# Two blocks of tokens scattered per step at the end of a chunk, and its slabs begun sooner: a GRU followed by a mixture of experts on one Trainium2 core

## The chip, the cores and the metric

The kernel runs on one core of a Trainium2 chip. The metric is the device time of one execution in microseconds, the median of several runs. The core has a matrix engine (PE), a vector engine (DVE), a scalar engine (ACT), a general engine (POOL) and a sync engine (SP). In this kernel SP issues nearly all plain DMAs, and POOL issues the indirect ones, whose rows are addressed by an index tile. Each engine takes its instructions in the order in which the program has them; an instruction that waits holds back all that stand behind it on that engine.

## The reference

A GRU runs over 256 time steps for 16 sequences of width 512. Each of the 4096 hidden states then goes through 8 low-rank experts of rank 128, of which two are kept, weighted by a normalised softmax of a router. The result is added to the input.

```python
def cell(h, x):
    gi = x @ W_ih + b_ih
    gh = h @ W_hh + b_hh
    i_r, i_z, i_n = jnp.split(gi, 3, axis=-1)
    h_r, h_z, h_n = jnp.split(gh, 3, axis=-1)
    r = jax.nn.sigmoid(i_r + h_r)
    z = jax.nn.sigmoid(i_z + h_z)
    n = jnp.tanh(i_n + r * h_n)
    h_new = (1.0 - z) * n + z * h
    return (h_new, h_new)
...
router_logits = x / norm @ router_w
routing_weights = softmax(router_logits)
rw, selected_experts = jax.lax.top_k(routing_weights, 2)
rw = rw / jnp.sum(rw, axis=-1, keepdims=True)
combine = sum over the two of one_hot(selected_experts, 8) * rw
out = sum over e of combine[:, e, None] * (x @ Wa[e] @ Wb[e])
x = x + out
```

## The kernel before

**The recurrence.** The outer loop has 32 blocks of 8 time steps; step `now` counts from 1 to 256. A step (function `step`) multiplies the hidden state by `W_hh` on PE into the banks `rn` (L914) and `z` (L924). ACT computes `r` (L940), `z` (L945) and `n` (L949), DVE the products around them (L947, L948, L952, L954, L956), and a DVE transpose (L959) turns the new state into `hist`, the left side of the next step's matmuls. Beside it PE multiplies the inputs of a later pair of steps by `W_ih` (L281, L289). ACT copies biases into the banks ahead of that (`seed`, L261). For the twelve pairs of steps in `EARLY` the input products are computed far ahead (class `Early`), so that in those steps PE has more time for the experts. Inputs are loaded a block at a time, eight DMAs on SP (`load_x`, L132).

**The experts.** The first 29 blocks are grouped in four chunks of 7, 11, 7 and 4 blocks. A block is 128 tokens. The last three blocks take a dense path over all experts (class `Moe`). For a block of a chunk, class `Route` issues these, a step or more apart: `keep` stores the block's states to DRAM (`H`, eight DMAs on SP, L597); `fetch` loads them back as rows of tokens (`ht`, on SP, L605), in the same piece as the router's logits; `norm` has ACT square and sum them (L620) and POOL take the root by a power (`nrm`, L622); `soft1` is the softmax on DVE and ACT; `soft2` picks two experts on DVE (`top2`; POOL fills the end of its tile `pr` by a memset, L319, before DVE's max, L324, may read it).

After the last block of a chunk, class `Chunk` places its tokens. It ranks them by expert (`ranks`, `places`, `experts`, `weights`, on PE and DVE). Then it moves every block's tokens into slots sorted by expert: `fetch(m)` loads the 128 tokens of block m from `H` into one of two `ht2` buffers (a 256 KB DMA on SP, L545), and `scatter(m)` writes them to the DRAM tensor `x_slots`, once for each of the two experts (two indirect DMAs on POOL, L551). `fetch(m + 2)` needs the buffer of block m back, so it waits until both scatters of m have landed.

The slots are then worked through in slabs of 128 (class `Slab`): four DMAs on SP load one (`xg`, L652), when all scatters of the chunk have landed; POOL copies its expert's weights (`wag`, `wbg`, L670, L674); DVE transposes it (L680); PE multiplies it down (L691) and up (L706) in four half pieces; ACT copies the result out (L714) and SP stores it (L715). When a chunk's slabs are done, class `Combine` gathers two rows per token (POOL, L743), loads the residual `xr` (SP, L739), adds both (DVE, L757) and stores the output (SP, L761).

**The planner.** Each of these classes gives a list of `Piece`s in its `plan`: a gap in steps to the piece before it, a cost in microseconds of PE, the PE work, the other operations (`then`), and the buffers it takes and gives. In each step `choose` takes what may come, in the order of `place`: chunks and routing at 0, in the order in which they began, slabs next, combines, dense blocks, early inputs last. Slabs and dense blocks have a due step, and a running credit spreads their cost up to it. PE work goes behind the step's own matmuls, the other operations behind the step's end. All engines' orders are then fixed as written. `ready[c]` is the step at which chunk c's slabs begin, and a chunk's slabs are due at `ready[c + 1] + 5`:

```python
ready = [e + LAG + k for e, k in zip(ends, CHUNKS)]
```

After step 256 the planner goes on, with more PE work per step, until all is done.

Of the kernel before, what the change touches and what calls it, by code (L numbers as in the profile page):

```python
# [23 lines left out]
CHUNKS = [7, 11, 7, 4]  # L24
LAG = 10
# [19 lines left out]
def gru_moe_kernel(  # L45
# [49 lines left out]
    E, _, R = wa.shape  # L95
# [263 lines left out]
    class Early:  # L359
# [55 lines left out]
        def plan(self):  # L415
            pieces = [
                Piece(then=[("load",)], takes="early"),
                Piece(gap=2, then=[("turn",)], takes="at"),
            ] + [
                Piece(gap=0, cost=c, pe=[("into", what, q)])  # L420
                for what, c in (("rn", 0.43), ("z", 0.22))
                for q in range(NQ)
            ] + [Piece(then=[("store",)], gives="early")]
            pieces[2].gap, pieces[2].takes = 1, ["ps"]
            pieces[9].then, pieces[9].gives = [("keep",)], ["ps", "at"]
            return pieces


    class Chunk:
# [139 lines left out]
        def plan(self):  # L569
            k = self.k  # L570
            pieces = [
                Piece(gap=7, cost=0.9, pe=[("ranks",)],
                      then=[("places",), ("places2",)]),
                Piece(then=[("places3",)]),
                Piece(then=[("experts",)]),
                Piece(then=[("weights",)]),
            ] + [Piece() for _ in range(k - 2)]
            pieces[0].then[:0] = [("fetch", m) for m in range(2)]
            for m in range(k):
                pieces[2 + m].then.append(("scatter", m))  # L580
                if m + 2 < k:
                    pieces[2 + m].then.append(("fetch", m + 2))
            return pieces

    class Route:
# [414 lines left out]
    starts = {}  # L1000
    room = dict(ROOM)
    ends = [TS * sum(CHUNKS[: c + 1]) for c in range(len(CHUNKS))]
    ready = [e + LAG + k for e, k in zip(ends, CHUNKS)]
    n_slabs = [(2 * P * k + (P - 1) * E) // P for k in CHUNKS]

    def at_step(n, make):
# [99 lines left out]
    for i in range(NB):  # L1106
        rows, rows_next = rows_next, None
        for t in range(TS):
# [3 lines left out]
            m = i * NM + t // 2  # L1112
# [20 lines left out]
        if i < n_sparse:  # L1133
            ch = chunks[-1]
            k = i - (ends[ch.c] // TS - ch.k)
# [55 lines left out]
```

## Time and profile before

| | us |
|---|---|
| median of 3 runs | 1308.48 (1308.43 to 1308.65) |
| the profiled execution | 1301.67 |
| its span, first to last instruction | 1299.9 |
| PE, DVE, ACT, POOL busy | 1252.2, 734.4, 391.4, 285.4 |
| first `r` (L940) of the recurrence, and last | 37.26, 1216.89 |
| last matmul ends | 1289.84 |

The mean granted clock of PE was 0.992. All times in the profile are of one execution and count from its first instruction. A line of the timeline gives the start, the duration, the engine, the source line, the operation, what it writes and reads, how many instructions it stands for, and in brackets how long the engine was idle before it and what ended that wait. A line of the waits names the waiting engine and line, what it waited for, and the total, the number and the longest of these waits. SPq is SP's queue of DMA issues: the duration there is that of issuing, not of the transfer.

### The profile page before, as it was taken

The numbers are of one execution on the slowest core, as the hardware profiler recorded it, in microseconds if no ns is written. First come the engines' busy times: TensorE is split into PE (matmuls) and PEld (weight loads), VectorE is DVE, ScalarE is ACT, GpSimd is POOL, SyncE is SP. The second block draws the span as 40 slices with busy tenths as digits, with TensorE's granted clock in tenths as the row PEclk, the third lists the DMA queues.
The fourth block names the chain that finished last, engine by engine and source line by source line (L and its number), as shares of the span: only waits on it lengthen the run. The fifth ranks groups of instructions, "written<-read, shape, count | busy, mean of one in ns | idle before, by whom it ended". The sixth has DMA issues, their size and how long they took to land. (4 is left out here: it accounts for less than half of the span.)

```text
span 1299.9 us, 68450 instructions
## 1 busy us (share of the span) xinstructions
PE 1252.2 (96%) x30378; PEld 888.0 (68%) x30378; DVE 734.4 (56%) x2678; ACT 391.4 (30%) x1354; POOL 285.4 (22%) x504
## 2 busy tenths in 40 slices
PE   6799999999999999999999999999999999999996
PEld 2477777777777777777777766777777777777652
DVE  1445555555555555555556646666556556676643
ACT  1222232222223333233232323333333333333320
POOL 2000000000421100000100433232114234373552
PEclk7999999999999999999999999999999999999999
DMA  8522322321522221112111544655335446774786
GB/s 196 158 98 86 103 91 80 104 92 47 191 77 62 60 61 54 49 44 60 43 56 57 193 153 122 173 163 150 97 98 184 150 134 183 207 224 144 206 256 179
DMA packets 149477, 158.67 MB, mean 122 GB/s; under 512 B 22646, under 2 KB 103606, under 8 KB 149180
## 3 DMA queue, kind: packets, MB, share of 16 engines
q1 hardware_dynamic: 139760, 123.83, 32.2%
q0 software_dynamic: 9280, 30.42, 7.5%
q8 instruction: 238, 3.90, 1.3%
q14 instruction: 59, 0.48, 0.1%
q10 hardware_dynamic: 140, 0.05, 0.0%
HBM read 84.21 MB, written 69.99 MB: 119 GB/s over the span
## 5 line engine op out<-in xcount | busy, mean ns | idle before, releaser
L914 PE MATMUL rn<-whh,hist 128*32 128x256 f32 x8160 | 493.6, 382 | 19.4 <-DVE hist L959 16.5
L914 PEld LDWEIGHTS rn<-whh,hist 128*32 128x32 f32 x8160 | 247.7, 110 | 201.4 <-DVE hist L959 51.8
L281 PE MATMUL rn<-wih,xT 128*32 128x256 f32 x3712 | 287.9, 381 | 11.3 <-DMA wih<-in_L_cond_W_ih_dram 9.4
L947 DVE SCALAR_TENSOR_TENSOR n<-r,rn 128x128 f32<-128x128 f32 x256 | 73.2, 286 | 362.2 <-ACT r L940 361.2
L924 PE MATMUL z<-whh,hist 128*32 128x128 f32 x8160 | 271.0, 273 | 0.0
L924 PEld LDWEIGHTS z<-whh,hist 128*32 128x32 f32 x8160 | 235.5, 110 | 42.9 <-issue 0.4
L940 ACT ACTIVATE r<-rn 128x128 f32<-128x128 f32 x256 | 70.9, 277 | 426.4 <-PE rn L914 426.4
L289 PE MATMUL z<-wih,xT 128*32 128x128 f32 x3712 | 188.4, 274 | 0.0
L289 PEld LDWEIGHTS z<-wih,xT 128*32 128x32 f32 x3712 | 122.0, 111 | 80.4 <-issue 1.8
L281 PEld LDWEIGHTS rn<-wih,xT 128*32 128x32 f32 x3712 | 112.0, 110 | 12.9 <-DMA wih<-in_L_cond_W_ih_dram 5.1
L945 ACT ACTIVATE z<-z 128x128 f32<-128x128 f32 x256 | 71.0, 278 | 151.1 <-PE z L924 150.5
L952 DVE SCALAR_TENSOR_TENSOR zh<-z,h 128x128 f32<-128x128 f32 x255 | 77.7, 305 | 65.6 <-ACT z L945 65.4
L622 POOL TENSOR_TENSOR nrm<-ss,half 128x1 f32<-128x1 f32 x29 | 16.2, 560 | 411.5 <-ACT ht L620 392.4
L691 PE MATMUL at_ps<-xgT,wag 128*32 128x128 f32 x2752 | 96.8, 273 | 2.2 <-POOL nrm L808 1.4
L706 PE MATMUL y_ps<-wbg,at 128*32 128x256 f32 x1376 | 94.6, 380 | 0.8 <-ACT at L698 0.8
L691 PEld LDWEIGHTS at_ps<-xgT,wag 128*32 128x32 f32 x2752 | 79.1, 110 | 9.8 <-issue 3.1
L959 DVE STREAM_TRANSPOSE hist<-rows 128x128 f32<-128x128 f32 x256 | 79.8, 312 | 8.7
L967 DVE STREAM_TRANSPOSE h<-hist 128x128 f32<-128x128 f32 x256 | 79.7, 311 | 8.7
L956 DVE SCALAR_TENSOR_TENSOR rows<-zh,m 128x128 f32<-128x128 f32 x256 | 76.0, 297 | 8.9
L674 POOL COPY wbg<-wb_sb 128x512 f32 x86 | 55.4, 644 | 114.9 <-PE y_ps L706 114.9
L949 ACT ACTIVATE n<-n 128x128 f32<-128x128 f32 x256 | 77.3, 302 | 7.6 <-DVE n L948 7.3
L714 ACT COPY y<-y_ps 128x512 f32<-128x512 f32 x86 | 50.1, 583 | 94.9 <-PE y_ps L706 85.7
(136 smaller groups left out, 1050.4 us busy)
## 6 DMA issues: line engine op xcount, KB each, us to landing
xg<-x_slots SPq DMA_DIRECT2D x344, 64.0 KB
y_slots<-y SPq DMA_DIRECT2D x86, 256.0 KB
ht<-H SPq DMA_DIRECT2D x58, 256.0 KB
x_slots<-zero SPq DMA_DIRECT2D x50, 256.0 KB
x<-in_x_dram SPq DMA_DIRECT2D x256, 32.0 KB
xr<-in_x_dram SPq DMA_DIRECT2D x32, 256.0 KB
out_dram<-xr SPq DMA_DIRECT2D x32, 256.0 KB
H<-rows SPq DMA_DIRECT2D x232, 32.0 KB
```

The source lines that it names most:

```text
L281: pe.matmul(rn[32 * j : 32 * j + 32, 0 : 3 * P].rearrange("p (g d) -> p g d", g=3)[:, 0:3:2, :], lhsT=xts[m][:, q, :], rhs=w[:, 0:3:2, j, ...
L289: ins = pe.matmul(zb[32 * j : 32 * j + 32, 0:P], lhsT=xts[m][:, q, :], rhs=w[:, 1, j, :], start=False, stop=(q == NQ - 1), skip_group_chec ...
L691: pe.matmul(self.ps[c32, 0:P], lhsT=self.wa[:, q, c32], rhs=self.xt[:, q, :], start=(q == 0), stop=(q == NQ - 1),)
L706: pe.matmul(self.ps[c32, half], lhsT=self.at[:, c32], rhs=self.wb[:, half], start=True, stop=True,)
L914: pe.matmul(rn[32 * j : 32 * j + 32, 0 : 2 * P].rearrange("p (g d) -> p g d", g=2), lhsT=hT[:, q, :], rhs=w(q, j)[:, 0:3:2, :], start=Fals ...
L924: pe.matmul(zb[32 * j : 32 * j + 32, 0:P], lhsT=hT[:, q, :], rhs=w(q, j)[:, 1, :], start=False, stop=(q == NQ - 1), skip_group_check=True,)
L947: dve.scalar_tensor_tensor(n, r, 1.0, rn[:, P : 2 * P], ALU.add, ALU.mult)
L949: act.activation(n, n, AF.Tanh)
L952: dve.scalar_tensor_tensor(zh, z, 1.0, hrow, ALU.add, ALU.mult)
L956: dve.scalar_tensor_tensor(hn, zh, 0.5, m, ALU.mult, ALU.subtract)
L959: dve.transpose(hist[:, t, :, lo : lo + 32], hn.rearrange("p (q c) -> p q c", q=NQ))
L967: dve.transpose(hrow.rearrange("p (q c) -> p q c", q=NQ), hT)
```

## The change

The scatters of two blocks, with the two fetches that reuse their buffers, now stand in one piece, where each block had a piece of its own. The plan of a chunk of k blocks has (k + 1) // 2 - 2 empty pieces behind the first four instead of k - 2. A chunk's slabs begin k - (k + 1) // 2 steps sooner: 3, 5, 3 and 2 steps. The due step of each chunk's slabs moves with the next chunk's start.

```diff
-            ] + [Piece() for _ in range(k - 2)]
+            ] + [Piece() for _ in range((k + 1) // 2 - 2)]
             pieces[0].then[:0] = [("fetch", m) for m in range(2)]
             for m in range(k):
-                pieces[2 + m].then.append(("scatter", m))
+                pieces[2 + m // 2].then.append(("scatter", m))
                 if m + 2 < k:
-                    pieces[2 + m].then.append(("fetch", m + 2))
+                    pieces[2 + m // 2].then.append(("fetch", m + 2))
             return pieces
...
-    ready = [e + LAG + k for e, k in zip(ends, CHUNKS)]
+    ready = [e + LAG + (k + 1) // 2 for e, k in zip(ends, CHUNKS)]
```

The two operations that are moved, as they stand in the kernel:

```python
def fetch(self, k):
    ht = moe.tile([P, D], FP, tag="ht2", bufs=2, name=f"ht2_{self.c}_{k}")
    sp.dma_start(ht, self.rows[k].rearrange("b t d -> (b t) d"))
...
def scatter(self, k):
    for ix in self.idx:
        ins = pool.indirect_dma_start(
            out=self.x[:, :],
            out_offset=bass.IndirectOffsetOnAxis(ap=ix[:, k : k + 1], axis=0),
            in_=self.ht[k][:, :],
...
```

## The prediction

> **What bounds the kernel now.** I read the page first, then the waits, then the timeline row by row at the end of each chunk, then the chain. The page and the two longest waits on ACT and DVE:
>
> ```profile
> PE 1252.2 (96%) x30378; PEld 888.0 (68%) x30378; DVE 734.4 (56%) x2678; ACT 391.4 (30%) x1354; POOL 285.4 (22%) x504
> ACT r L940 <- PE rn L914: 426.4, 248, 3.9
> DVE n L947 <- ACT r L940: 361.2, 237, 4.9
> ```
>
> PE has work nearly always, and the recurrence hands each of the 256 steps on in turn (PE, ACT `r`, DVE `n`, ACT, DVE, PE). The starts of `r` (L940) run from 37.26 to 1216.89 us. With at most one half slab piece (cost 0.43 in the plan) a step takes 4.41 us; two take 4.77, three 5.20, four about 5.65. So beside the input-gate matmuls a step lasts about max(4.41, 3.91 + cost): the loop has some 0.5 us of free PE time, and all beyond is paid. ACT and DVE obey their own order: whatever makes either wait stops the step.
>
> What the change touches is not on PE. Waits on POOL and on SP's queue (total us, times, longest):
>
> ```profile
> POOL x_slots L551 <- DMA ht<-H: 49.8, 16, 6.9
> SPq L545 <- DMA x_slots<-ht,ilo: 57.9, 12, 12.6
> ```
>
> POOL's scatter waits for its block's fetch, SP's fetch waits for a scatter. It is a loop through the two `ht2` buffers: scatter m must have landed before fetch m+2 may be issued, and that before scatter m+2. The timeline of POOL and SP in chunk 1:
>
> ```profile
> 717.01 1.04 POOL L551 DMA_INDIRECT x_slots<-ht,ihi  x1 [8.31 <-DVE ilo L507]
> 718.36 0.99 POOL L551 DMA_INDIRECT x_slots<-ht,ilo  x1 [0.30 <-issue]
> ...
> 726.10 1.00 POOL L551 DMA_INDIRECT x_slots<-ht,ihi  x1 [3.09 <-DMA ht<-H]
> ...
> 735.74 0.59 POOL L622 TENSOR_TENSOR nrm<-ss,half 128x1 f32<-128x1 f32 x1
> ...
> 743.48 0.14 POOL L319 MEMSET pr<- 128x6 f32 x1
> 722.35 0.32 SPq L545 DMA_DIRECT2D ht<-H  x1
> 722.77 5.46 SPq L597 DMA_DIRECT2D H<-rows  x8
> ```
>
> Scatter 0 leaves POOL at 719.35, fetch 2 is issued at 722.35 (3.0 us), scatter 2 starts at 726.10 (3.75 us). Over the chunk the first gap lies between 1.8 and 3.3 us, the second between 3.55 and 5.1, long beside the H stores. I take 2.6 and 3.9 (5.0 beside H stores). With 2.25 us of POOL for a pair of scatters the loop takes 2.25 + 2.6 + 3.9 = 8.75 us for two blocks, 4.4 a block: just the length of a step. The old plan, one block a step, is already at that rate. And the loop once stops the recurrence, at step 164 (7.31 us between its `r` and the next), when the next block's `ht` fetch stood behind it on SP:
>
> ```profile
> 773.17 0.63 ACT L620 ACTIVATE ht<-ht 128x512 f32<-128x512 f32 x1 [4.14 <-DMA ht<-H]
> ```
>
> **The change part by part.** The number of scatters, fetches, matmuls and bytes is the same. Two blocks a step are asked of a loop that yields one. By the order of the changed program's instructions, a chunk's queues look so: on SP, fetches 2 and 3 now precede the next block's eight H stores (L597), fetches 4 and 5 its `ht` fetch (L605), 8 and 9 (of the 11-block chunk) an x load. On POOL, the next block's `nrm` power (L622) stands behind scatter 6 (chunks 0, 2) or 7 (chunk 1) instead of behind 3; its `pr` memset (L319) in chunk 1 behind scatter 10 instead of 5. ACT's Square (L620) waits for that `ht`, DVE's softmax for `nrm`, DVE's max (L324) for `pr`; ACT and DVE are the recurrence.
>
> *Chunk 1 (11 blocks).* From scatter 0 at 717.0: fetch 2 at 722.35, fetch 3 at 724.5, H stores 724.9 to 730.4 (5.5 us as in the row), fetch 4 at 731.0; scatter 3 at 729.6 to 731.9, fetch 5 at 734.5, the `ht` fetch at 734.9, landing at 737.5 (it took 2.6 us before: 731.30 to 733.87). ACT then needs 2.35 us for Square, a `y` copy and the seeds: `r` of step 157 at 739.85 in place of 736.8, 3.05 us lost. Scatters 4 to 7 start at 734.9, 738.4, 743.7, 747.2, so `nrm` is ready at 750.2 and `n` of step 158 starts at 751.5, not 741.46: 10.0 us lost in all. Scatters 8, 9 and 10 end at 754.8, 758.3 and 764.0 (fetch 10 waits for SP's x load until 757.8). Then `pr`, 0.95 us of top-two on DVE, and `n` of step 159 at 765.3 in place of 745.88. **+19.4 us.** The stall at step 164 goes, because the block's fetch then finds SP free: 7.31 to 4.41, **-2.9.**
>
> *Chunk 0 (7 blocks).* Fetch 2 at 328.4 and scatter 2 at 332.2 as now; fetch 3 331.7, H stores to 338.0, fetch 4 338.0, fetch 5 341.1, `ht` fetch 341.5, landing 344.4 against 341.25: 3.1 us. Scatter 4 from 341.9 to 344.2, fetch 6 346.8, scatter 6 from 350.7 to 353.0, `nrm` 353.6, softmax 1 us: `n` of step 70 at 354.8 in place of 347.7. **+7.1.**
>
> *Chunk 2 (7 blocks).* The same chain from 982.28 brings `nrm` to 1012.2. But these steps carry slab work and take 5.1 to 5.6 us, so the recurrence comes later and waits less: `ht` costs 0.5, `nrm` 3.5. **+4.0.**
>
> *Chunk 3 (4 blocks)* has no routed block behind it; scatter 3 now ends near 1155.5, and the slab weights behind it on POOL (near 1157) are needed by PE near 1166. **0**, with bounds -1 (a 5.94 us step near there loses its excess) and +2 (one weight late).
>
> *Slabs begun sooner.* The plan now begins them at steps 71, 161, 215, 245 in place of 74, 166, 218, 247. Summing max(4.41, 3.91 + cost) over both plans (2.18 in place of 3.91 where no input gates are computed) gives 5.2 us more in the recurrence; the work after step 256 falls from 66.7 to 62.4, and PE is busy there nearly throughout (L863, L826, L691, L706 end to end), so 4.3 comes back. **+0.9.** This is the whole PE effect of the head start: work moved from one full place to another.
>
> *The end.* PE's last matmul ended at 1289.84, but the span at 1299.9. The chain says why:
>
> ```profile
> 1282.81 5.35 DMA out_dram<-xr
> 1288.15 0.02 issue
> 1288.17 4.24 DMA xr<-in_x_dram
> ```
>
> The last residual tile was loaded late, behind two Combine outputs, and Combines 27 and 28 ended after it. In the new plan these two stand 3 steps before, but the last `xr` load still waits behind their outputs on SP. From the starting time of the last block's routing I get 18.2 us to its landing (Combine outputs 5.35, loads 4.24, adds 0.74 each) against 16.4 for PE, then 0.7 and 4.6 us for add and output: 23.6 where it now is 26.4. **-2.8**, bounds -5 (load not late at all) and 0.
>
> The trace cannot show two pairs of scatters with two fetches issued in one step. From below, transfers could be no slower than the shortest gaps (1.8 and 3.55: loop 7.6 us), from above they crowd (3.3 and 4.7: 10.3 us). A rule weighs against my size: the Trainium skill, "DMA: Bandwidth & Descriptors", section "Anatomy of one DMA", puts a DMA at about 2.0 us plus its bytes at 436 GB/s. For 256 KB that is an estimate of 2.6 us, so 2.25 + 2.6 + 2.6 = 7.45 us a loop. The first gap agrees, the second is measured at 3.75 where the rule says 2.6. By the rule chunk 1 would lose 12.5, chunk 0 3, chunk 2 0.5, and the sum be +11. I take the rows, and keep the rule as the near end.
>
> Sum: 7.1 + 19.4 - 2.9 + 4.0 + 0 + 0.9 - 2.8 = **+25.7 us.** The profiled execution took 1301.67 us (span 1299.9), 6.8 under the median of the runs, 1308.48; I carry the difference over: 1334.2.
>
> **The rivals.**
> - *Short loop.* Fetches in pairs land as the rule says: +11, 1319.5. For it: gaps of 1.8 us occur. Against: the second gap was never under 3.55.
> - *Long loop.* Scatters, fetches, H stores and x loads crowd one another at 10.3 us a loop or more: 1.6 us more per loop, five loops in chunk 1 (8 us), three in chunk 0 (5) and three in chunk 2 (some 3, the rest hidden), so 16 more, 1350. For it: 5.1 us beside the H stores.
> - *Faster: the queue does not hold.* If POOL never waited for a fetch, a pair would cost it 2.55 us, 11 blocks 28 us, and `pr` would be ready at 745, when DVE wants it. Then only -2.9, +0.9 and -2.8 remain: -4.8, 1303.7. It decides from a loop under some 5.1 us for two blocks; every row speaks for over 7.
> - *No head start at all.* The slabs begin 3 to 5 steps sooner, but these steps come later on the clock: step 161 would be at 773.8, step 166 was at 779.3. In that case the -2.8 at the end falls away too: 1337. It is within the forecast's range.
>
> **How the numbers follow.** Forecast with its near variant 0.74, short loop 0.11, long loop 0.09, faster 0.03, no difference (short loop and a full gain at the end) 0.03. Low 1318 takes in the rule, high 1347 the larger part of the long loop. About 0.2% (2.6 us) is what a measurement of this kernel can tell from no change: faster 0.03, same 0.03, slower 0.94.
>
> **What would show it.** In the profile after: POOL waiting for `ht<-H` before most scatters, for 3 to 5 us; `nrm` (L622) and `pr` (L319) directly behind a scatter; DVE waiting for `nrm` near steps 69, 157 and 213, and for `pr` at step 158, by about 7 and 9 us in chunk 1; the 7.31 us step gone; PE's share of the span lower. Wrong would be: no DVE wait for POOL at these steps, a loop under 7 us, or chunks 0 to 2 longer by less than 10 us in all.

## The result, and the profile after

| | before | after |
|---|---|---|
| median of six runs each, us | 1308.57 (1305.98 to 1310.31) | 1346.22 (1342.87 to 1348.98) |
| profiled execution, us | 1301.67 | 1346.27 |
| its span, us | 1299.9 | 1344.5 |
| mean granted clock of PE | 0.992 | 0.978 |

The ratio is 1.0298 (1.0282 to 1.0314); the two medians stand 37.7 us apart, where 25.7 were forecast. The profiled executions stand 44.6 apart, because that of before lay 7 us under its median and that of after did not; below, the terms are those of the profiled executions.

The page and the waits of the kernel after (total us, times, longest), and below them two waits of the kernel before:

```profile
PE 1264.1 (94%) x30378; PEld 894.9 (67%) x30378; DVE 738.3 (55%) x2678; ACT 391.7 (29%) x1354; POOL 286.6 (21%) x504
POOL x_slots L551 <- DMA ht<-H: 49.0, 16, 6.6
DVE rn L301 <- POOL nrm L622: 19.0, 3, 8.3
DVE m L324 <- POOL pr L319: 17.9, 3, 13.1
ACT ht L620 <- DMA ht<-H: 11.9, 3, 5.7
```

```profile
ACT ht L620 <- DMA ht<-H: 6.4, 4, 4.1
DVE m L324 <- POOL pr L319: 1.3, 2, 0.8
```

The first wait, POOL on the fetches, is as long as before (49.8). What has changed is who waits for POOL and SP in turn: DVE for `nrm` and `pr`, ACT for `ht`. Together these waits are 48.8 us, three times each. Before, ACT's wait for `ht` was 6.4 us, DVE's for `pr` 1.3, and one for this `nrm` was not in the list. The timeline of POOL and DVE in chunk 1 (start, duration, engine, line, what; in brackets the idle time before):

```profile
759.98 0.97 POOL L551 DMA_INDIRECT x_slots<-ht,ilo  x1 [0.30 <-issue]
760.97 0.59 POOL L622 TENSOR_TENSOR nrm<-ss,half 128x1 f32<-128x1 f32 x1
...
776.57 0.97 POOL L551 DMA_INDIRECT x_slots<-ht,ihi  x1 [6.61 <-DMA ht<-H]
777.85 0.97 POOL L551 DMA_INDIRECT x_slots<-ht,ilo  x1 [0.31 <-issue]
778.79 0.15 POOL L319 MEMSET pr<- 128x6 f32 x1
761.59 0.15 DVE L301 TENSOR_SCALAR rn<-nrm 128x1 f32<-128x1 f32 x1 [8.34 <-POOL nrm L622]
...
778.97 0.17 DVE L324 MAX8 m<-pr 128x8 f32<-128x14 f32 x1 [13.08 <-POOL pr L319]
```

A memset of 0.15 us, queued behind the eleventh scatter, holds DVE for 13.08 us and with it the recurrence. The small instructions that the forecast named stand where it put them. Not in the forecast is what the idle time does to PE. Four stretches of 6 us in chunk 1 (length, then busy PE, PEld, DVE, ACT, POOL with their instructions; granted clock, DMA share, GB/s):

```profile
730.00:736.00 6.00, 6.00 (x184) 4.67 (x180) 4.63 (x19) 0.75 (x3) 2.17 (x3) 1.00 0.60 187
760.00:766.00 6.00, 2.22 (x32) 1.38 (x36) 3.50 (x15) 1.95 (x8) 3.00 (x4) 0.51 0.59 157
778.00:784.00 6.00, 1.57 (x16) 0.79 (x20) 3.53 (x16) 0.31 (x1) 2.36 (x5) 0.50 0.23 87
790.00:796.00 6.00, 6.00 (x160) 4.55 (x156) 1.98 (x7) 1.73 (x7) 0.00 (x0) 1.00 0.26 77
```

In the two stretches with a stall the granted clock was 0.51 and 0.50, in the two others 1.00. The timeline of PE has it at the next state product:

```profile
782.43 3.64 PE L914 MATMUL rn<-whh,hist 128*32 128x256 f32 x32 [11.82 <-DVE hist L959]
```

The same 32 matmuls take 1.93 us elsewhere. The kernel before has one such slow product, near its start:

```profile
65.51 3.02 PE L914 MATMUL rn<-whh,hist 128*32 128x256 f32 x32 [3.78 <-DVE hist L959]
```

The end has a queue of its own. POOL, then DVE and PE, in the last dense block, and below them the same last product in the kernel before:

```profile
1325.71 1.00 POOL L743 DMA_INDIRECT yg<-y_slots,ilo  x1 [0.30 <-issue]
1326.69 0.13 POOL L319 MEMSET pr<- 128x6 f32 x1
1326.86 0.18 DVE L324 MAX8 m<-pr 128x8 f32<-128x14 f32 x1 [4.66 <-POOL pr L319]
1328.81 1.97 PE L847 MATMUL aT_ps<-ident,a 128*128 128x128 f32 x8 [6.74 <-DVE a L838]
1330.70 8.46 PE L863 MATMUL o_ps<-wb_sb,aT 128*32 128x512 f32 x64
```

```profile
1282.76 7.08 PE L863 MATMUL o_ps<-wb_sb,aT 128*32 128x512 f32 x64
```

The gathers of Combines 27 and 28 now stand ahead of this block's `pr` on POOL. PE idles 6.74 us and then takes 8.46 us for the product that took 7.08 before. The two Combines are early now, and the end after the last matmul is 5.3 us instead of 10.1; but the last matmul itself comes late.

### The profile page after: what moved, and what is told of

It is laid out like the page before. It is cut to its first block, busy times and chain, and to the rows that moved or that the text cites. A ratio compares the mean times of both kernels' runs of the same rounds, so it can differ in the third digit from the quotient of the medians.

```text
span 1344.5 us, 68453 instructions
## 1 busy us (share of the span) xinstructions
PE 1264.1 (94%) x30378; PEld 894.9 (67%) x30378; DVE 738.3 (55%) x2678; ACT 391.7 (29%) x1354; POOL 286.6 (21%) x504
## 4 chain that ended last, share of the span: by engine, by line
PE 79%; DMA 8%; issue 5%; DVE 3%; POOL 2%; SPq 1%; ACT 1%; POOLq 0%; ACTq 0%; DVEq 0%
PE rn L914 31%; PE z L924 15%; PE rn L281 13%; PE z L289 6%; PE y_ps L706 4%; PE at_ps L691 4%; DMA x_slots<-ht,ilo 3%; DMA ht<-H 2%; PE gi L387 1%; POOL x_slots L551 1%; DMA wih<-in_L_cond_W_ih_dram 1%; DMA whh<-in_L_cond_W_hh_dram 1%; PE rt L353 1%; POOL yg L743 1%; DMA wb_sb<-in_L_ffn_Wb_dram 1%
## 5 line engine op out<-in xcount | busy, mean ns | idle before, releaser
L914 PE MATMUL rn<-whh,hist 128*32 128x256 f32 x8160 | 499.6, 386 | 31.4 <-DVE hist L959 29.4
L914 PEld LDWEIGHTS rn<-whh,hist 128*32 128x32 f32 x8160 | 252.1, 111 | 216.1 <-DVE hist L959 63.5
L281 PE MATMUL rn<-wih,xT 128*32 128x256 f32 x3712 | 289.3, 383 | 14.6 <-ACT rn L261 7.4
L281 PEld LDWEIGHTS rn<-wih,xT 128*32 128x32 f32 x3712 | 112.2, 111 | 16.5 <-ACT rn L261 8.2
L948 DVE SCALAR_TENSOR_TENSOR n<-n,rn 128x128 f32<-128x128 f32 x256 | 73.6, 287 | 8.7
```

Of the source, the lines that this page charges most:

```text
L281: pe.matmul(rn[32 * j : 32 * j + 32, 0 : 3 * P].rearrange("p (g d) -> p g d", g=3)[:, 0:3:2, :], lhsT=xts[m][:, q, :], rhs=w[:, 0:3:2, j, ...
L914: pe.matmul(rn[32 * j : 32 * j + 32, 0 : 2 * P].rearrange("p (g d) -> p g d", g=2), lhsT=hT[:, q, :], rhs=w(q, j)[:, 0:3:2, :], start=Fals ...
L948: dve.scalar_tensor_tensor(n, n, 0.5, rn[:, 2 * P : 3 * P], ALU.mult, ALU.add)
```

## The experiments

Eight kernels were run in two groups of four, each group beside the kernel before on the same chip. The median of before was 1307.84 in the first group and 1306.83 in the second; ratios are to it. "In chunk 0, 1, 2" gives what the steps 65 to 71, 153 to 160 and 209 to 215 lost against the profiled execution of before, from the starts of `r`; the changed kernel itself lost 11.4, 26.1, 7.5.

**The slabs late again, the scatters still in pairs.**

```diff
-    ready = [e + LAG + (k + 1) // 2 for e, k in zip(ends, CHUNKS)]
+    ready = [e + LAG + k for e, k in zip(ends, CHUNKS)]
```

> The scatters in pairs, the slabs begun as late as before. Theory (in-order queues: the paired scatter loop keeps POOL and SP from the next block's small instructions, so DVE and ACT, and with them the recurrence, stand still): the steps behind chunks 0, 1, 2 lose about what they lose in the changed kernel, 11 + 25 + 7.5 us in the profile; what is left of the changed kernel's loss, the end, goes back to that of the kernel before: about 1340 to 1344 us. Rival (the sooner slabs crowd PE and the DMA queues): most of the loss goes, below 1325 us.

Measured: 1340.95, ratio 1.0256 (1.0239 to 1.0273); in chunk 0, 1, 2: 11.0, 21.1, 10.7. The rival falls: 33 of the 38 us come with the pairs alone. Chunk 1 loses 5 us less than in the changed kernel, chunk 2 3 us more. The end is back to that of before (PE's last matmul 73.0 us after the last `r`, the rest 10.5; before 72.95 and 10.06).

**The fill of `pr` on DVE**, in `top2`:

```diff
-        pool.memset(pr[:, E:14], 2.0)
+        dve.memset(pr[:, E:14], 2.0)
```

> The changed kernel, with the fill of the tail of pr (L319) on DVE instead of POOL. Theory (queues): the wait of 13.1 us of DVE for pr in chunk 1 goes, a softmax wait of 8.3 us stays; at the end DVE no longer waits 4.7 us for pr behind the gathers, so PE no longer 6.7 us for the last scale; chunks 0 and 2 stay. In all 18 to 24 us less, about 1324 us. Rival (the DMA loop itself has to be awaited by someone): the later slabs or the next stage take up the time, over 1338 us.

Measured: 1329.48, ratio 1.0164 (1.0137 to 1.0192), so 16.7 less than the changed kernel, a little under the forecast. Chunk 1 falls from 26.1 to 13.0, chunks 0 and 2 stay near (10.4, 6.0), and the end is 3.7 us shorter. DVE's wait for `nrm` remains (16.7 us in three, longest 8.6). The rival falls: the time is not taken up elsewhere, the wait was the cost.

**Four token buffers instead of two**, in `Chunk.fetch`:

```diff
-            ht = moe.tile([P, D], FP, tag="ht2", bufs=2, name=f"ht2_{self.c}_{k}")
+            tag, bufs = ("ht2", 2)
+            if self.c < 3 and k % 4 > 1:
+                tag, bufs = (("aT", 1), ("a", 1))[k % 4 - 2]
+            ht = moe.tile([P, D], FP, tag=tag, bufs=bufs, name=f"ht2_{self.c}_{k}")
```

> The changed kernel, with four token buffers for the scatters of chunks 0 to 2 instead of two (two further tiles, idle until the dense blocks, serve); same instructions, same order. Theory: the loop has four blocks under way, so POOL's own 2.55 us per block sets the pace; the waits of DVE for nrm and pr in chunks 0 to 2 nearly vanish (40 us less, of which about 3 may stay in chunk 1): 1305 to 1312 us. Rival (POOL's issuing and the DMA engines' speed is what is short): scatters still 4.4 us apart, over 1335 us.

Measured: 1316.03, ratio 1.0061 (1.0037 to 1.0084); in chunk 0, 1, 2: 1.1, 10.4, 2.0. The losses of chunks 0 and 2 nearly vanish. POOL in chunk 1 of this kernel (the first scatter of a pair only; `...` where pairs are left out):

```profile
721.49 1.04 POOL L554 DMA_INDIRECT x_slots<-ht,ihi  x1 [0.30 <-issue]
724.12 0.98 POOL L554 DMA_INDIRECT x_slots<-ht,ihi  x1 [0.30 <-issue]
726.68 0.97 POOL L554 DMA_INDIRECT x_slots<-ht,ihi  x1 [0.30 <-issue]
732.51 0.97 POOL L554 DMA_INDIRECT x_slots<-ht,ihi  x1 [3.58 <-DMA ht<-H]
...
742.47 0.59 POOL L625 TENSOR_TENSOR nrm<-ss,half 128x1 f32<-128x1 f32 x1
...
751.72 0.97 POOL L554 DMA_INDIRECT x_slots<-ht,ihi  x1 [3.59 <-DMA ht<-H]
753.95 0.14 POOL L319 MEMSET pr<- 128x6 f32 x1
```

One block's pair of scatters can follow the last by 2.6 us: two buffers, not POOL and not the DMA engines, were what held the loop at over 4 us a block. It came out 4 us above the expected band, since `pr` still waits for fetch 10, which stands behind an x load on SP (6.8 us of DVE's waiting where 3 were expected), and for the gathers at the end, where PE still idles 6.3 us in one wait.

**PE kept at work in the stalls.** `fill(0)` and `fill(1)` stand before and after the first `gate_in` of a step, `fill(2)` behind the step's PE work (these three calls are left out below). The numbers in `FILL` come to 30 groups of eight matmuls, where the expectation says 27:

```diff
+    FILL = {(0, 69): 3, (0, 157): 3, (1, 70): 3, (1, 158): 6, (1, 214): 3, (2, 159): 12}
+
+    def fill(where):
+        n = FILL.get((where, now), 0)
+        if n:
+            idle = big(f"fill_{where}_{now}")
+            for _ in range(n):
+                for j in range(NJ):
+                    pe.matmul(
+                        idle[32 * j : 32 * j + 32, :], lhsT=zero[:, 0:32], rhs=zero,
+                        start=True, stop=True,
+                    )
```

> The changed kernel, with matmuls of zeros (27 groups of about 0.86 us) put on PE where it stands still in chunks 0 to 2; they write to a bank that nobody reads. Theory (part of the loss is PE coming back from idleness at a low granted clock): the slow matmuls behind the stalls, 3.64, 2.72, 3.64 and 3.35 us for rn where 1.93 is usual, return to 1.93: 5 to 7 us less, about 1340 us. Rival (the waits are all of it): no change, or up to 3 us more where the filler outlasts a wait.

Measured: 1341.43, ratio 1.0259 (1.0238 to 1.0279), 4.8 less than the changed kernel, with more work on PE. The interval ends just below that of the changed kernel (1.0282). The timeline of PE, at the place of the 3.64 us row shown above:

```profile
767.56 10.48 PE L1007 MATMUL fill<-zero 128*32 128x512 f32 x96
779.04 1.93 PE L914 MATMUL rn<-whh,hist 128*32 128x256 f32 x32 [0.99 <-DVE hist L959]
```

All four slow products in the chunks are back to 1.93 or less. Chunk 0 loses 9.2, chunk 1 21.3. Chunk 2 lost more than without the filler (9.7; one product ahead of the filler took 2.51 us), so no gain is shown there. The DVE waits (`nrm` 15.7, `pr` 16.6) stayed: this term adds to them. The Trainium skill ("TensorE: Matmul & The Clock Gate", section "What's actually happening") says that the array falls to half its clock after an idle window of about 3.4 us, in windows that run freely. PE in the kernel after:

```profile
345.45 0.64 PE L281 MATMUL rn<-wih,xT 128*32 128x256 f32 x8 [3.43 <-ACT rn L261]
...
355.24 0.65 PE L289 MATMUL z<-wih,xT 128*32 128x128 f32 x8 [3.41 <-ACT z L945]
...
357.05 3.64 PE L914 MATMUL rn<-whh,hist 128*32 128x256 f32 x32 [0.30 <-DVE hist L959]
...
750.46 1.08 PE L281 MATMUL rn<-wih,xT 128*32 128x256 f32 x8 [2.73 <-ACT rn L261]
```

The rows agree in part: after 3.43 us of idleness the next products kept full speed, after 3.41 us they did not. But 2.73 us of idleness was enough once: the eight matmuls of L281 behind it took 1.08 us where 0.64 or less is usual, at a granted clock of 0.50. So the length of the wait alone did not decide, and 3.4 us was not a lower bound.

**Routing ahead of the scatters within a step**, with `pr` on DVE:

```diff
-        pool.memset(pr[:, E:14], 2.0)
+        dve.memset(pr[:, E:14], 2.0)
...
-                begin(ch, 0)
+                begin(ch, 0.5)
```

> The changed kernel with the fill of pr on DVE, and the chunk's scatters and fetches placed behind the next block's routing within a step (its place is 0.5 instead of 0): H stores and the ht fetch then stand ahead of the chunk's fetches on SP, the power for nrm ahead of scatter 6 on POOL. The scatter loop stays as slow as it is. Theory (it is the order, not the loop): the ACT waits for ht go, of the waits of DVE for nrm at most 4 us stay in chunk 0 and 2 in chunk 1: 1309 to 1315 us. Rival (the loop's time has to be paid whatever stands first): over 1322 us, as with the fill of pr on DVE alone.

Measured: 1316.36, ratio 1.0064 (1.0039 to 1.009); in chunk 0, 1, 2: 5.6, 6.3, 6.9. Another 13 us go with the same slow loop (POOL still waits 50.6 us for fetches). The rival falls, but the theory was too hopeful: in all three chunks the scatter before `nrm` is still late, and DVE waits for `nrm` 13.8 us in all. ACT's wait for `ht` falls to 4.7 us.

**All three together**:

```diff
-        pool.memset(pr[:, E:14], 2.0)
+        dve.memset(pr[:, E:14], 2.0)
...
-            ht = moe.tile([P, D], FP, tag="ht2", bufs=2, name=f"ht2_{self.c}_{k}")
+            tag, bufs = ("ht2", 2)
+            if self.c < 3 and k % 4 > 1:
+                tag, bufs = (("aT", 1), ("a", 1))[k % 4 - 2]
+            ht = moe.tile([P, D], FP, tag=tag, bufs=bufs, name=f"ht2_{self.c}_{k}")
...
-                begin(ch, 0)
+                begin(ch, 0.5)
```

> The changed kernel with all three: pr filled on DVE, routing ahead of the scatters within a step, four token buffers in chunks 0 to 2. Theory: no step behind a chunk's end is longer by over 1 us; the recurrence as long as before the change, less the 2.9 us of step 164; the end no longer than in the run with pr on DVE alone: 1302 to 1309 us. Rival (two blocks a step load the DMA engines or POOL too much in any order): over 1313 us.

Measured: 1300.02, ratio 0.9931 (0.991 to 0.9951), 2 us under the expected band. In chunk 0, 1, 2: 0.4, -0.8, 2.0. Two of its waits:

```profile
POOL x_slots L554 <- DMA ht<-H: 23.4, 7, 7.2
DVE rn L301 <- POOL nrm L625: 0.9, 1, 0.9
```

DVE's wait for `pr` and ACT's for `ht` are gone from the list. Two blocks a step cost nothing that can be measured once nobody stands behind them.

**The same with the slabs late**; beside the last diff:

```diff
-    ready = [e + LAG + (k + 1) // 2 for e, k in zip(ends, CHUNKS)]
+    ready = [e + LAG + k for e, k in zip(ends, CHUNKS)]
```

> The same with the slabs begun as late as before the change. It tells what the head start is worth when no stall hides it. Theory (the work is moved from one full place on PE to another): within 3 us of the run before it, either way. Rival (the head start is the gain that the stalls ate): 4 us or more slower than with the head start.

Measured: 1299.04, ratio 0.9936 (0.9917 to 0.9955). The head start is worth nothing that can be measured. In the profiles it makes the last `r` 5.2 us later (1218.48 against 1213.31), and the stretch from there to the end of the span 2.4 us shorter (80.3 against 82.7).

**The kernel before with the same three**; beside the last two diffs:

```diff
-            ] + [Piece() for _ in range((k + 1) // 2 - 2)]
+            ] + [Piece() for _ in range(k - 2)]
...
-                pieces[2 + m // 2].then.append(("scatter", m))
+                pieces[2 + m].then.append(("scatter", m))
                 if m + 2 < k:
-                    pieces[2 + m // 2].then.append(("fetch", m + 2))
+                    pieces[2 + m].then.append(("fetch", m + 2))
```

> The kernel before the change, one block a step, with the same three: pr on DVE, routing first, four buffers. Theory: only the stall at step 164 (2.9 us) and a part of the small ones go: 1302 to 1307 us, no more than 3 us from the run with pairs. Rival (pairs are worth something once the queues are clear): 4 us or more slower than the kernel with pairs and all three.

Measured: 1298.97, ratio 0.9935 (0.9917 to 0.9954), 3 us under the expected band. The pairs bring nothing either; the three kernels are one within their intervals. Each is faster than the changed kernel, and than the kernel before by 6.8 us or more.

## Why the prediction was right or wrong

The direction, the place and the chain of causes were right. The size was not. The median, 1346.2, lies just under the far end of the range, 1347; of 44.6 us between the profiled executions the sum had 25.7. Two steps of the sum failed: the terms of the chunks, too short by 14.5 us, and the time given back after step 256, which did not come (-4.3 forecast, +6.9 measured). The other terms came out 6.8 us better than forecast.

| term | forecast | measured |
|---|---|---|
| chunk 0 | 7.1 | 11.4 |
| chunk 1 | 19.4 | 26.1 |
| chunk 2 | 4.0 | 7.5 |
| the other steps (head start 5.2, step 164 -2.9) | 2.3 | -2.6 |
| last `r` to last matmul | -4.3 | 6.9 |
| last matmul to the end | -2.8 | -4.7 |

- *The terms of the chunks* were 14.5 us short. Two parts of that are seen. The loop was put at 8.75 us for two blocks; in chunk 1 it took 8.6, 10.45, 8.4, 9.0 and 12.3, or 9.8 on average. The last is the largest: fetch 10 was issued at 769.74, behind eight x loads and one more small load, and its scatter started 6.8 us later, where 3.9 were assumed. So scatter 10 ended 51 us after the first began, not 47. And PE's clock behind the stalls was put at nothing, though the row at 65.51 stood in the trace of before. `fill` shows 4.8 us for it; in chunk 0 the step behind the stall (step 70) took 6.00 us, and 4.30 with the filler. The rest of the 14.5 is not split.
- *"PE is busy there nearly throughout, so 4.3 comes back"* failed, by 11.2 us, the largest single error. PE from the last `r` to its last matmul, before and after (as in the table of stretches above):

```profile
1216.89:1289.84 72.95, 69.74 (x1160) 36.21 (x1149) 33.03 (x75) 15.54 (x39) 38.67 (x52) 1.00 0.81 238
1259.29:1339.16 79.87, 66.92 (x1056) 34.68 (x1045) 34.71 (x75) 13.91 (x35) 35.09 (x46) 0.96 0.70 204
```

The work did fall, by about a hundred matmuls. But PE idled 13.0 us there instead of 3.2. The forecast followed the Combines on SP and DVE, and `pr` in chunk 1 only; at the end the same memset stands behind moved gathers, and PE waits 6.74 us for it. With `pr` on DVE the last matmul came 75.3 us after the last `r` instead of 79.9, though still not before the 72.95 of the old order. PE waits there 2.5 us for the `nrm` of a dense block, which POOL computes when DVE, held by a late `xr`, has given it `lg`, and 1.8 us for the last scale.
- *The head start as work moved*: where no stall hides it, the last `r` is 5.2 us later, as forecast (4.7 counted from the first `r`). Of that, 2.4 came back by the end, not 4.3. In the changed kernel step 164 fell from 7.31 to 4.40 us, as forecast, so that only some 0.3 of the 5.2 shows outside the three chunks; a part lies inside them (step 71 took 5.26 us, and 4.41 with the slabs late).
- *The near end, a loop by the rule of the skill (7.45 us)*, fell: in chunk 1 scatters 2, 3, 4, 6, 8 and 10 started 3.8 to 6.8 us after their fetch was issued, and the rule has 2.6. The section that the prediction names in the Trainium skill ("DMA: Bandwidth & Descriptors", "Anatomy of one DMA") is about transfers that POOL issues. The fetches are issued by SP, so the rule bore on the first gap alone, and the measured rows were the right choice for the second.
- *The long loop* came true for the two worst loops of chunk 1 alone. *Faster* fell as forecast. *No head start* named the right outcome for the end, which gained nothing, but not the way.
- *The carried 6.8 us* was wrong for the kernel after, whose profiled execution is at its median. By luck it hid 7 us of the shortfall; without it the forecast median would have stood at 1327.4.

What stays open: the old pace with all three edits is 7.9 us under the median of before, but only 3.6 us between the spans of the profiled executions, 2.6 of them in steps 161 to 208, where step 164 lies. Where the other 4 us come from was not traced.

## What to carry to other kernels

When two moves of a transfer loop are put into one step, list every small instruction that now stands behind them on each in-order queue, and ask for each who waits for it; do it at every place where the order moves, the end too. Work out the loop from its buffers first: in the changed kernel two buffers gave one block in 4.1 us at best, a step took 4.4, and asking for two blocks a step only lengthened the queue. A tiny fill or power on a queue that waits for transfers belongs ahead of the transfers, or, as was tried here for the fill, on the engine that reads it.

## What was not expected of the hardware

The price of a stall does not end with it. In the kernel after, 32 matmuls of the state product took 2.72 to 3.64 us instead of 1.93 behind PE's waits of 3.4 to 11.8 us in the chunks; the granted clock was 0.50 to 0.51 in such stretches, and zeros on PE during the waits brought the products back to 1.93 in chunks 0 and 1. In the last block, the final product took 8.46 us instead of 7.08 after 6.74 us of idleness.
